# Turning a mixture's tokens and slot rows by VectorE and SBUF transfers, and three evictions given to ScalarE

## The chip, the cores and the metric

The kernel runs on one core of a Trainium2 chip. The metric is the device time of one execution in microseconds (us). A core has five engines that run their own instruction queues in order and wait for each other by semaphores: TensorE (PE; its weight loads are shown as PEld), VectorE (DVE), ScalarE (ACT), GpSimd (POOL) and SyncE (SP), which in this kernel issues every transfer (DMA). SBUF is the on-chip memory; TensorE writes its results to PSUM, from which VectorE or ScalarE moves them (an eviction).

## What is computed

Two layers over x of shape (2, 1024, 256) in fp32, each of a cross-attention to a context of 64 rows and a feed-forward, with a residual sum around each:

```python
x = x + L0_xattn(layernorm(x), ctx)   # 8 heads, softmax within 4 windows of 16 keys
x = x + L0_ffn(layernorm(x))          # 8 groups of 256 tokens: (x W1^T + b1) W2^T + b2
x = x + L1_xattn(layernorm(x), ctx)   # 16 heads of 16, sigmoid scores
x = x + L1_ffn(layernorm(x))          # mixture, below

# L1_ffn(x): slot_embeds of shape (8, 128, 256) = 1024 slot rows
xn = rms_norm(x, gamma_x);  se = rms_norm(slot_embeds, gamma_slot)
logits = einsum('bsd,etd->bset', xn, se)
dispatch = softmax(logits, axis=1)             # over the tokens
slots = einsum('bsd,bset->betd', xn, dispatch)
processed = gelu(slots @ w1) @ w2
combine = softmax(logits over all 1024 slots)  # over the slots
out = einsum('bnd,bsn->bsd', processed, combine)
```

The change concerns the way to logits: the product over d needs both tokens and slot rows with d on the partitions, so both are transposed ("turned").

## The kernel before

The 2048 tokens are held as four quads (q = 0 to 3, two to a batch), each a tile x of 128 partitions x 4 token tiles x 256. Stages follow each other:

- **Layer 0** (to about 107 us). The eight groups' weight pairs are multiplied ahead into one 256x256 matrix each (`product`, L522, tile pmt), with bias sums by VectorE (`bias_rows`, L553, tile b2z). Between the products stand `weigh` (scores psc L729, maximum mx L739, difference e L741, exponential L746, weights at L751), `attend` (transposes pat L760 of the weights, their eviction atT L762, product po L767, sum into x L775), `norm_ff` and `feed_forward` (po L580, POOL's bias sum L574, sum into x L587).
- **Layer 1's attention** (about 107 to 176 us). Keys and values are made once and evicted into kblk (L862) and vblk1 (L885). Then for every quad q and each of two chunks c: scores psg (L957, four banks), tanh by ScalarE (L966, tile sg), and, after what the code puts in between, the product poT (L996) and its eviction oT (L1003). In between stand the next quad's layer norm (`layernorm`, transposes pt_a L125) and queries (pq L897), the last quad's output (pf L911, sum into x L919), and the mixture's preparation.
- **The mixture's preparation.** `norm_slots` makes the slot rows' sums of squares (ScalarE, L826), their square root by POOL's pow (L829), and scales the rows by VectorE (L834). `turn_slot_rows(dc, h)` transposes four 128x128 blocks on TensorE (pse L842) and evicts them with the product of the two gammas into seT (L843). `norm_tokens(q)` takes moments by VectorE, powers by POOL (L117, L159), a few small VectorE operations (L160 to L165) and four scalings (L169) into xh. `turn_tokens(q)` transposes eight blocks on TensorE (pt_m L180) and evicts them by ScalarE and VectorE into xhT (L150, L152).
- **Logits** (about 170 to 236 us). Unit u = 0 to 15 is a tile of 128 tokens: four products pl (L196; each fp32 product is two instructions), VectorE's minimum and running maximum (L204, L211, L215), ScalarE's exponential ec (L219). Quads 0 to 3 are read from u = 0, 4, 8 and 12 on. `largest` (L254) and `spread` (L273) make the slot maxima's rows mb, and POOL adds them (`less`, L278).
- **Slots, hidden layer, combine** (236 us to the end), for each batch: `gather` (psl L289), `hidden` (pmh L364), `processed` (pp L430), `combine` (pc L455, sum into x L462, output L466). Meanwhile `turn` turns the exponentials ec by VectorE's 32x32 block transposes (L236, tile tr) and 16 transfers within SBUF (L243), each of 32 partitions; the weights ms are loaded (L1050).

The order of instructions on each engine is planned at build time by the library: it simulates the program with its own estimates and takes, of the instructions that are ready in its simulation, the one that comes first in the program. `nc.any` leaves the choice between ScalarE and VectorE to it. From the end of layer 1 on ScalarE follows the program's order. `tc.keep_in_program_order(i)` lets i be queued only behind the instruction that stands before it in the program on the same engine; it adds no wait. PSUM tiles come from two rotations (sides) of four banks.

Of the kernel before, what the change touches and what calls it, by code (L numbers as in the profile page):

```python
# [21 lines left out]
QT = 4  # L22
# [28 lines left out]
def tile_kernel(  # L51
# [10 lines left out]
    wff_in: bass.AP,  # L62
    b2: bass.AP,
    gammas: bass.AP,
    w1_in: bass.AP,
# [28 lines left out]

    gxs = const.tile([P, 2, DC], FP, name="gxs")
    gx, gs = gxs[:, 0, :], gxs[:, 1, :]
    ggx = const.tile([P, DC], FP, name="ggx")

# [6 lines left out]
    )  # L105
    seT = const.tile([P, DC, NSLOT], FP, tag="seT", name="seT")

    def moments(xt, name):

        st = stat.tile([P, QT, 6], FP, tag="bn", name=f"bn_{name}")  # L110
        mv = stat.tile([P, QT, 2], FP, tag="mv", name=f"mv_{name}")
        for t in range(QT):
            nc.vector.bn_stats(st[:, t, :], xt[:, t, :])
            nc.vector.bn_aggr(mv[:, t, :], st[:, t, :])
        rstd = stat.tile([P, QT], FP, tag="rstd", name=f"rstd_{name}")
        nc.gpsimd.tensor_scalar(rstd, mv[:, :, 1], LN_EPS, None, ALU.add)
        nc.gpsimd.tensor_tensor(rstd, rstd, m_half, ALU.pow)  # L117
        return mv, rstd

    def transposed(src, dst, name, side=0):  # L120

        for c in range(DC):
            pt = bank(f"pt_{name}_{c}", side)
            for t in range(QT):
                nc.tensor.transpose(pt[:, ts(t, P)], src[:, t, ts(c, P)], ident)  # L125
            nc.any.tensor_copy(dst[:, c, :], pt)


# [24 lines left out]

    def norm_tokens(q):

        mv, rstd = moments(xq[q], f"m_{q}")

        f = stat.tile([P, QT], FP, tag="f", name=f"f_{q}")
        nc.gpsimd.tensor_tensor(f, mv[:, :, 1], p_half, ALU.pow)  # L159
        nc.vector.tensor_scalar(f, f, float(D) ** 0.5, None, ALU.mult)  # L160
        nc.vector.tensor_tensor(f, f, rstd, ALU.mult)
        nc.vector.tensor_scalar(f, f, RMS_EPS, None, ALU.max)
        nc.vector.reciprocal(f, f)
        nc.vector.tensor_tensor(f, f, rstd, ALU.mult)
        nc.vector.tensor_scalar(f, f, float(D) ** 0.5, None, ALU.mult)  # L165
        xh = keep[q // QB].tile([P, QT, XW], FP, tag=f"xh_{q % QB}", name=f"xh_{q}")
        nc.gpsimd.memset(xh[:, :, D:XW], 1.0)
        for t in range(QT):
            nc.vector.tensor_scalar(  # L169
                xh[:, t, 0:D], xq[q][:, t, :], mv[:, t, 0:1], f[:, t : t + 1],  # L170
                ALU.subtract, ALU.mult,
            )
        xhs[q] = xh

    def turn_tokens(q):
        xhT = pools["mw"].tile([P, DC, QN], FP, tag="xhT", name=f"xhT_{q}", bufs=2)
        for c in range(DC):
            pt = bank(f"pt_m_{q}_{c}", 1)
            for t in range(QT):
                nc.tensor.transpose(pt[:, ts(t, P)], xhs[q][:, t, ts(c, P)], ident)  # L180
            copy(c, xhT[:, c, :], pt)
        xhTs[q] = xhT

    def logits(b, s):
# [8 lines left out]
        for n in range(NSLOT // 512):  # L193
            pl = bank(f"pl_{b}_{s}_{n}", 0)
            for dc in range(DC):
                nc.tensor.matmul(  # L196
                    pl,
                    lhsT=xhTs[q][:, dc, ts(t, P)],
                    rhs=seT[:, dc, ts(n, 512)],
                    start=(dc == 0),  # L200
                    stop=(dc == DC - 1),
                )
# [265 lines left out]
    with (  # L468
# [5 lines left out]
        se = w1p.tile([P, EC, D], FP, name="se")  # L474

        NCT, NPE = DC * 2 * B * NK, DC * NK
        fr = w1p.tile([P, NCT + NPE + NG * OC], FP, name="fr")
# [113 lines left out]
        def load_layer1():  # L591
            nc.sync.dma_start(out=w1s, in_=w1_in)
            nc.sync.dma_start(out=se, in_=slots_in)
            nc.sync.dma_start(out=gxs, in_=gammas)

        with tc.tile_pool(name="p0", bufs=1) as p0, tc.tile_pool(name="a0", bufs=2) as a0:
# [159 lines left out]
            def attend(q):  # L756
# [4 lines left out]
                atT = a0.tile([P, QN], FP, tag="atT", name=f"atT_{q}")  # L761
                nc.any.tensor_copy(atT, pat)  # L762
                for i in range(2):
# [51 lines left out]
        with (  # L815
# [3 lines left out]

            def norm_slots():  # L820
                sq = a1c.tile([P, D], FP, name="sq")
                sn = a1c.tile([P, EC], FP, name="sn")
                p_half8 = a1c.tile([P, EC], FP, name="p_half8")
                nc.gpsimd.memset(p_half8, 0.5)
                for c in range(EC):
                    nc.scalar.activation(  # L826
                        sq, se[:, c, :], AF.Square, accum_out=sn[:, c : c + 1]
                    )
                nc.gpsimd.tensor_tensor(sn, sn, p_half8, ALU.pow)  # L829
                nc.vector.tensor_scalar(sn, sn, RMS_EPS, None, ALU.max)  # L830
                nc.vector.reciprocal(sn, sn)
                nc.vector.tensor_scalar(sn, sn, float(D) ** 0.5, None, ALU.mult)
                for c in range(EC):
                    nc.vector.tensor_scalar(  # L834
                        se[:, c, :], se[:, c, :], sn[:, c : c + 1], None, ALU.mult
                    )
                nc.vector.tensor_tensor(ggx, gx, gs, ALU.mult)

            def turn_slot_rows(dc, h):
                pt = bank(f"pse_{dc}_{h}", 1)  # L840
                for c in range(4):
                    nc.tensor.transpose(pt[:, ts(c, P)], se[:, 4 * h + c, ts(dc, P)], ident)  # L842
                nc.vector.tensor_scalar(  # L843
                    seT[:, dc, ts(h, 512)], pt, ggx[:, dc : dc + 1], None, ALU.mult
                )

# [13 lines left out]
            for c in range(C1):  # L860
                for e in range(2):
                    nc.vector.tensor_scalar(  # L862
                        kblk[:, c, :, e, :],
                        pk[:, ts(c, P)].rearrange("p (b s) -> p b s", b=B),
                        parity[:, e : e + 1],
                        None,
                        ALU.mult,
                    )
# [14 lines left out]
            for e in range(2):  # L883
                r = slice(e * NK, (e + 1) * NK)
                nc.vector.tensor_copy(vblk1[r, :, :, e, :], pvv[r, :, :, e, :])  # L885

# [63 lines left out]
            for q in range(NQ):  # L950
                b = q * QN // S
                oTs[q] = a1.tile([P, C1, QN], FP, tag="oT", name=f"oT_{q}")
                for c in range(C1):
# [15 lines left out]
                    if c == 0:  # L969
# [11 lines left out]
                        if q > 0:  # L981
                            output(q - 1, (0, 1) if q + 1 < NQ else (0,))
                            turn_slot_rows(*divmod(q - 1, 2))
                        if q + 1 == NQ:
                            turn_tokens(0)
                    elif q + 1 < NQ:
                        queries(q + 1)
                        if q + 2 == NQ:
                            norm_tokens(0)
                            turn_slot_rows(1, 1)  # L990
                    else:
# [23 lines left out]
    for u in range(1, B * ST + 2):  # L1015
        b, s = divmod(u, ST)
        if b < B:
            if s % QT == 1:
                q = u // QT + 1
                if q < NQ:  # L1020
                    norm_tokens(q)
            logits(b, s)
            if s % QT == 2:
                q = u // QT + 1
                if q < NQ:
                    turn_tokens(q)
        v = u - ST
# [115 lines left out]
```

## Time and profile before

| | |
|---|---|
| median of 3 runs | 462.3 us (461.98 to 462.48) |
| profiled execution: time, span | 461.42 us, 459.6 us |
| TensorE busy | 446.4 us, 97% of the span |
| VectorE busy | 261.1 us, 57% |
| ScalarE busy | 110.8 us, 24% |
| POOL busy | 84.9 us, 18% |
| transfers | 38.61 MB, mean 84 GB/s |
| granted TensorE clock | 1.0 throughout |

A profile is one execution. "Busy" is the sum of an engine's instructions; the matmuls overlap each other, so the duration of one is longer than its distance from the next. The chain that ended last is followed back from the last instruction, at each step to what released it or to the instruction before it on its engine; it gives that distance. In the lists, L522 is line 522 of the kernel, "pmt<-wg" is output from input, and "idle" with an arrow names what ended an engine's wait.

### The profile page before, as it was taken

How to read it: one execution, taken by the hardware profiler on the slowest of the kernel's cores; microseconds unless marked ns; L12 is line 12 of the kernel's file. 1: busy time of each engine (PE TensorE's matmuls, PEld its weight loads, DVE VectorE, ACT ScalarE, POOL GpSimd, SP SyncE). 2: the span in 40 equal slices, each digit the busy share in tenths (PEclk: the TensorE clock that was granted, in tenths of full speed). 3: DMA queues.
4: the chain of work that ended last, by engine and by line, in shares of the span. 5: the costliest groups of instructions: out<-in, count | busy, mean ns of one | idle time of the engine just before them, and what ended most of it. 6: DMA issues, size and time to landing. Idle time of an engine off the chain costs nothing.

```text
span 459.6 us, 5446 instructions
## 1 busy us (share of the span) xinstructions
PE 446.4 (97%) x2032; PEld 322.2 (70%) x2032; DVE 261.1 (57%) x623; ACT 110.8 (24%) x205; POOL 84.9 (18%) x84
## 2 busy tenths in 40 slices
PE   6999897999999999999999999999999999999997
PEld 5788795888645555445458854688888874488886
DVE  0487889897256677987776279611331539911111
ACT  1212331211344441342573306300000003410000
POOL 3011332325111101100878910000000000000000
PEclk9999999999999999999999999999999999999999
DMA  8994691500000000000007534140252040430011
GB/s 287 411 429 198 260 427 45 185 0 1 1 1 0 2 0 1 0 0 1 0 1 227 89 52 72 33 80 0 52 98 36 12 79 1 82 102 1 11 47 35
DMA packets 74381, 38.61 MB, mean 84 GB/s; under 512 B 68465, under 2 KB 70641, under 8 KB 72945
## 3 DMA queue, kind: packets, MB, share of 16 engines
q1 hardware_dynamic: 74354, 38.26, 27.4%
q8 instruction: 16, 0.26, 0.2%
q14 instruction: 11, 0.09, 0.1%
HBM read 27.76 MB, written 2.10 MB: 65 GB/s over the span
## 4 chain that ended last, share of the span: by engine, by line
PE 82%; DVE 6%; POOL 1%; issue 0%
PE psl L289 12%; PE pc L455 12%; PE pp L430 12%; PE pl L196 11%; PE pmh L364 11%; PE pmt L522 6%; PE pq L897 3%; PE pf L911 3%; PE po L580 2%; PE psg L957 2%; PE poT L996 2%; DVE b2z L553 1%; DVE hn_f L486 1%; PE po L767 1%; PE pt_a L125 1%; PE pb L273 1%
## 5 line engine op out<-in xcount | busy, mean ns | idle before, releaser
L522 PE MATMUL pmt<-wg 128*128 128x256 f32 x256 | 60.1, 393 | 3.8 <-DMA wg<-in_wff_dram 3.8
L289 PE MATMUL psl<-xh,lg 128*128 128x258 f32 x256 | 58.7, 381 | 0.0
L522 PEld LDWEIGHTS pmt<-wg 128*128 128x128 f32 x256 | 49.9, 198 | 11.4 <-DMA wg<-in_wff_dram 4.3
L196 PE MATMUL pl<-seT,xhT 128*128 128x512 f32 x128 | 56.1, 592 | 0.0
L455 PE MATMUL pc<-pr,ec 128*128 128x256 f32 x256 | 55.6, 379 | 0.0
L430 PE MATMUL pp<-ms,mh 128*128 128x256 f32 x256 | 55.6, 379 | 0.0
L430 PEld LDWEIGHTS pp<-ms,mh 128*128 128x128 f32 x256 | 48.6, 190 | 7.5 <-DVE mh L408 0.5
L455 PEld LDWEIGHTS pc<-pr,ec 128*128 128x128 f32 x256 | 48.6, 190 | 6.6
L289 PEld LDWEIGHTS psl<-xh,lg 128*128 128x128 f32 x256 | 47.4, 190 | 7.2 <-issue 0.5
L196 PEld LDWEIGHTS pl<-seT,xhT 128*128 128x128 f32 x128 | 24.1, 190 | 27.9 <-issue 26.3
L278 POOL TENSOR_TENSOR lg<-lg,mb 128x1024 f32<-128x1024 f32 x16 | 37.2, 2366 | 32.3 <-ACT mb L150 27.9
L462 DVE SCALAR_TENSOR_TENSOR x<-pc,zc,x 128x256 f32<-128x256 f32 x16 | 7.7, 484 | 42.3 <-PE pc L455 42.3
L442 DVE COPY pr<-pp 128x512 f32<-128x512 f32 x8 | 5.5, 692 | 45.5 <-PE pp L430 45.5
L219 ACT ACTIVATE ec<-lg,nm 128x1024 f32<-128x1024 f32 x16 | 18.4, 1148 | 41.6 <-DVE nm L204 41.6
L398 ACT COPY mh<-pmh 128x512 f32<-128x512 f32 x8 | 4.6, 572 | 89.6 <-PE pmh L364 89.6
L374 ACT ACTIVATE mh<-mh 128x512 f32<-128x512 f32 x32 | 19.0, 626 | 21.1 <-DVE mh L408 16.1
L364 PE MATMUL pmh<-slT,ms 128*128 128x512 f32 x48 | 24.0, 592 | 0.0
L553 DVE SCALAR_TENSOR_TENSOR b2z<-wg,fr,b2z 128x256 f32<-128x256 f32 x48 | 23.6, 494 | 0.3
L297 DVE RECIPROCAL rz<-psl 128x1 f32<-128x1 f32 x16 | 2.6, 164 | 32.7 <-PE psl L289 32.7
L966 ACT ACTIVATE sg<-psg 128x512 f32<-128x512 f32 x32 | 16.5, 603 | 18.0 <-PE psg L957 18.0
L236 DVE STREAM_TRANSPOSE tr<-ec 128x512 f32<-128x512 f32 x32 | 20.1, 679 | 0.0
L281 ACT ACTIVATE lg<-lg 128x1024 f32<-128x1024 f32 x16 | 16.5, 1049 | 12.2 <-POOL lg L278 12.2
(169 smaller groups left out, 585.9 us busy)
## 6 DMA issues: line engine op xcount, KB each, us to landing
wg<-in_wff_dram SPq DMA_DIRECT2D x6, 2048.0 KB, 12.4
ec<-tr SPq DMA_DIRECT2D x128, 64.0 KB, 2.1
xT<-in_xT_dram SPq DMA_DIRECT2D x4, 512.0 KB, 13.4
x<-in_x_dram SPq DMA_DIRECT2D x4, 512.0 KB, 14.9
wg<-in_wff_dram SPq DMA_DIRECT2D x2, 1024.0 KB, 11.3
ms<-in_m_dram SPq DMA_DIRECT2D x1, 2048.0 KB, 8.3
out_dram<-x SPq DMA_DIRECT2D x16, 128.0 KB, 1.8
wg<-in_wff_dram SPq DMA_DIRECT2D x3, 512.0 KB, 6.0
```

What stands on the lines that cost most here:

```text
L196: nc.tensor.matmul(pl, lhsT=xhTs[q][:, dc, ts(t, P)], rhs=seT[:, dc, ts(n, 512)], start=(dc == 0), stop=(dc == DC - 1),)
L219: nc.scalar.activation(ecs[q][:, :, t, :], lg.rearrange("p (h n) -> p h n", h=2), AF.Exp, bias=nm[:, 1:2], scale=-1.0, accum_out=zcs[b][:, ...
L236: nc.vector.transpose(tr[:, :, :, t, :].rearrange("p r c n -> p c r n"), half[:, t, :].rearrange("p (c r n) -> p c r n", c=EC // 2, r=R4),)
L278: nc.gpsimd.tensor_tensor(lgs[b][s], lgs[b][s], mbs[b], ALU.add)
L281: nc.scalar.activation(lgs[b][s], lgs[b][s], AF.Exp, scale=-1.0)
L289: nc.tensor.matmul(pz[:, 0:XW], lhsT=lgs[b][s][:, ts(c, P)], rhs=xhs[b * QB + s // QT][:, s % QT, :], start=(s == 0), stop=(s == ST - 1),)
L364: nc.tensor.matmul(to, lhsT=lefts[i][:, ts(j, P)], rhs=slTs[b][:, i, 0:512] if i < 2 else rights[b][i], start=True, stop=True,)
L374: nc.scalar.activation(h, h, AF.Gelu)
L430: nc.tensor.matmul(pp[:, ts(k, D)], lhsT=hss[b, g, fc // 2][:, fc % 2, ts(2 * c2 + k, P)], rhs=m12s[1][:, fc, :], start=(fc == 0), stop=(f ...
L455: nc.tensor.matmul(pc[:, 0:D], lhsT=turned[:, c // 4, c % 4, t, :], rhs=prs[b, c // 4][:, c % 4, :], start=(c == 0), stop=(c == EC - 1),)
L522: nc.tensor.matmul(pm[:, ts(hc, D)], lhsT=w1g[:, oc, ts(hc, P)], rhs=w2g[:, oc, :], start=(oc == 0 and hc == 0), stop=(oc == OC - 1 and hc ...
L553: nc.vector.scalar_tensor_tensor(acc, weights[g][1][:, oc, :], b1s[:, g, oc : oc + 1], acc, ALU.mult, ALU.add)
```

## The change

Tokens and slot rows are no longer transposed on TensorE. A new helper `turned` does for 512 rows of 256 what `turn` does already for ec: four VectorE transposes of 32x32 blocks (128x256 each) into a tile tr, then 16 transfers within SBUF, issued by SP, that put the blocks in place (32 partitions x 8 runs of 128 bytes, 32 KB each). It is called four times for tokens and twice for slot rows, so the kernel has 24 more VectorE transposes and 96 more transfers, and 48 fewer TensorE transposes with their 12 evictions. Since nothing is evicted, the gammas go on the slot rows before: they are loaded as rows to all partitions (ggb), multiplied with each other and with each half of se by POOL; ScalarE scales the rows. seT is laid out half by half.

`norm_slots` and the slots' transposes are pinned in program order: behind the tanh of chunk (0,0), and behind layer 1's chunks (0,1) and (1,0). `norm_tokens` is split (`token_stats`); quads 0 and 1 are normed and turned in layer 1's chunks (1,1) and (2,1), quads 2 and 3 at logit units 1 and 3, and there is a third xhT buffer. Layer 1's keys and values, and layer 0's atT, are evicted by ScalarE. The host passes the gammas in two arrays: gx as before by partition, and both as rows.

```diff
     )
-    seT = const.tile([P, DC, NSLOT], FP, tag="seT", name="seT")
+    seT = const.tile([P, 2, DC, 512], FP, tag="seT", name="seT")
...
-        st = stat.tile([P, QT, 6], FP, tag="bn", name=f"bn_{name}")
-        mv = stat.tile([P, QT, 2], FP, tag="mv", name=f"mv_{name}")
+        st = stat.tile([P, QT, 6], FP, tag="bn" + name[0], name=f"bn_{name}")
+        mv = stat.tile([P, QT, 2], FP, tag="mv" + name[0], name=f"mv_{name}")
         for t in range(QT):
...
             nc.vector.bn_aggr(mv[:, t, :], st[:, t, :])
-        rstd = stat.tile([P, QT], FP, tag="rstd", name=f"rstd_{name}")
+        rstd = stat.tile([P, QT], FP, tag="rstd" + name[0], name=f"rstd_{name}")
         nc.gpsimd.tensor_scalar(rstd, mv[:, :, 1], LN_EPS, None, ALU.add)
...
+    def turned(src, dst, tr, late=False):
+        for t in range(QT):
+            turn = nc.vector.transpose(
+                tr[:, :, :, t, :].rearrange("p r c n -> p c r n"),
+                src[:, t, 0:D].rearrange("p (c r n) -> p c r n", c=DC, r=R4),
+            )
+            if late:
+                tc.keep_in_program_order(turn)
+        to = dst.rearrange("p c (t i n) -> p (c t) i n", t=QT, i=R4)
+        for i in range(R4):
+            for r in range(R4):
+                nc.sync.dma_start(
+                    out=to[ts(r, SQ), :, i, :],
+                    in_=tr[ts(i, SQ), r].rearrange("p c t n -> p (c t) n"),
+                )
...
-    def norm_tokens(q):
+    stats = {}
+    def token_stats(q):
         mv, rstd = moments(xq[q], f"m_{q}")
...
         nc.gpsimd.tensor_tensor(f, mv[:, :, 1], p_half, ALU.pow)
-        nc.vector.tensor_scalar(f, f, float(D) ** 0.5, None, ALU.mult)
+        stats[q] = mv, rstd, f
+    def norm_tokens(q):
+        if q not in stats:
+            token_stats(q)
+        mv, rstd, f = stats[q]
+        tc.keep_in_program_order(
+            nc.vector.tensor_scalar(f, f, float(D) ** 0.5, None, ALU.mult)
+        )
         nc.vector.tensor_tensor(f, f, rstd, ALU.mult)
...
     def turn_tokens(q):
-        xhT = pools["mw"].tile([P, DC, QN], FP, tag="xhT", name=f"xhT_{q}", bufs=2)
-        for c in range(DC):
-            pt = bank(f"pt_m_{q}_{c}", 1)
-            for t in range(QT):
-                nc.tensor.transpose(pt[:, ts(t, P)], xhs[q][:, t, ts(c, P)], ident)
-            copy(c, xhT[:, c, :], pt)
+        xhT = pools["mw"].tile([P, DC, QN], FP, tag="xhT", name=f"xhT_{q}", bufs=3)
+        tr = pools["mw"].tile([P, R4, DC, QT, SQ], FP, tag="tr", name=f"tr_m_{q}", bufs=2)
+        turned(xhs[q], xhT, tr)
         xhTs[q] = xhT
...
                     lhsT=xhTs[q][:, dc, ts(t, P)],
-                    rhs=seT[:, dc, ts(n, 512)],
+                    rhs=seT[:, n, dc, :],
                     start=(dc == 0),
...
+        ggb = w1p.tile([P, 2, D], FP, name="ggb")
         NCT, NPE = DC * 2 * B * NK, DC * NK
...
             nc.sync.dma_start(out=se, in_=slots_in)
-            nc.sync.dma_start(out=gxs, in_=gammas)
+            nc.sync.dma_start(out=gx, in_=gx_in)
+            nc.sync.dma_start(out=ggb, in_=gammas.partition_broadcast(P))
...
                 atT = a0.tile([P, QN], FP, tag="atT", name=f"atT_{q}")
-                nc.any.tensor_copy(atT, pat)
+                nc.scalar.copy(atT, pat)
                 for i in range(2):
...
             def norm_slots():
+                late = tc.keep_in_program_order
                 sq = a1c.tile([P, D], FP, name="sq")
...
                 p_half8 = a1c.tile([P, EC], FP, name="p_half8")
-                nc.gpsimd.memset(p_half8, 0.5)
+                late(nc.gpsimd.memset(p_half8, 0.5))
                 for c in range(EC):
-                    nc.scalar.activation(
-                        sq, se[:, c, :], AF.Square, accum_out=sn[:, c : c + 1]
+                    late(
+                        nc.scalar.activation(
+                            sq, se[:, c, :], AF.Square, accum_out=sn[:, c : c + 1]
+                        )
                     )
...
                 nc.vector.tensor_scalar(sn, sn, float(D) ** 0.5, None, ALU.mult)
+                gg = ggb[:, 0, :]
+                late(nc.gpsimd.tensor_tensor(gg, gg, ggb[:, 1, :], ALU.mult))
                 for c in range(EC):
-                    nc.vector.tensor_scalar(
-                        se[:, c, :], se[:, c, :], sn[:, c : c + 1], None, ALU.mult
-                    )
-                nc.vector.tensor_tensor(ggx, gx, gs, ALU.mult)
-            def turn_slot_rows(dc, h):
-                pt = bank(f"pse_{dc}_{h}", 1)
-                for c in range(4):
-                    nc.tensor.transpose(pt[:, ts(c, P)], se[:, 4 * h + c, ts(dc, P)], ident)
-                nc.vector.tensor_scalar(
-                    seT[:, dc, ts(h, 512)], pt, ggx[:, dc : dc + 1], None, ALU.mult
-                )
+                    nc.scalar.activation(
+                        se[:, c, :], se[:, c, :], AF.Copy, scale=sn[:, c : c + 1]
+                    )
+                for h in range(2):
+                    sh = se[:, ts(h, QT), :]
+                    nc.gpsimd.tensor_tensor(
+                        sh, sh, gg.unsqueeze(1).to_broadcast([P, QT, D]), ALU.mult
+                    )
+            def turn_slot_rows(h):
+                tr = lnp.tile([P, R4, DC, QT, SQ], FP, tag="tr", name=f"tr_se_{h}")
+                turned(se[:, ts(h, QT), :], seT[:, h], tr, late=True)
...
                 for e in range(2):
-                    nc.vector.tensor_scalar(
+                    nc.scalar.activation(
                         kblk[:, c, :, e, :],
                         pk[:, ts(c, P)].rearrange("p (b s) -> p b s", b=B),
-                        parity[:, e : e + 1],
-                        None,
-                        ALU.mult,
+                        AF.Copy,
+                        scale=parity[:, e : e + 1],
                     )
...
                 r = slice(e * NK, (e + 1) * NK)
-                nc.vector.tensor_copy(vblk1[r, :, :, e, :], pvv[r, :, :, e, :])
+                nc.scalar.copy(vblk1[r, :, :, e, :], pvv[r, :, :, e, :])
...
                             output(q - 1, (0, 1) if q + 1 < NQ else (0,))
-                            turn_slot_rows(*divmod(q - 1, 2))
-                        if q + 1 == NQ:
-                            turn_tokens(0)
+                        if q == 1:
+                            turn_slot_rows(1)
+                        if 0 < q < 3:
+                            token_stats(q - 1)
+                    if c == 1 and 0 < q < 3:
+                        norm_tokens(q - 1)
+                        turn_tokens(q - 1)
+                    if c == 0:
+                        pass
                     elif q + 1 < NQ:
                         queries(q + 1)
-                        if q + 2 == NQ:
-                            norm_tokens(0)
-                            turn_slot_rows(1, 1)
+                        if q == 0:
+                            turn_slot_rows(0)
                     else:
...
         if b < B:
-            if s % QT == 1:
-                q = u // QT + 1
-                if q < NQ:
-                    norm_tokens(q)
+            if u in (1, 3):
+                norm_tokens(QB + u // 2)
+                turn_tokens(QB + u // 2)
             logits(b, s)
-            if s % QT == 2:
-                q = u // QT + 1
-                if q < NQ:
-                    turn_tokens(q)
         v = u - ST
```

## The prediction

> **What bounds the kernel now.** I read the page's busy shares first, then TensorE's waits, then the chain that ended last, then the timelines of the engines that the change touches. Page, parts 1 and 2:
>
> ```profile
> PE 446.4 (97%) x2032; PEld 322.2 (70%) x2032; DVE 261.1 (57%) x623; ACT 110.8 (24%) x205; POOL 84.9 (18%) x84
> ...
> PE   6999897999999999999999999999999999999997
> ...
> PEclk9999999999999999999999999999999999999999
> ```
>
> TensorE is busy in 97% of the span, at the full granted clock. A busy row can hide short gaps, so I checked what TensorE waited for (us in total, times, longest):
>
> ```profile
> PE pmt L522 <- DMA wg<-in_wff_dram: 3.8, 1, 3.8
> PE po L767 <- DVE atT L762: 3.4, 1, 3.4
> PE pt_f L125 <- DVE e L741: 1.2, 1, 1.2
> PE pwk L686 <- ACT vblk L675: 1.0, 1, 1.0
> PE po L767 <- ACT atT L762: 0.7, 1, 0.7
> ```
>
> All of them lie before 73 us. The chain says the same: from 49.6 to 72.6 us it runs through VectorE, and from there nearly all is TensorE, back to back, to the last combine. So after 73 us each TensorE instruction that goes is worth its spacing, as long as nothing else comes late. The chain has the transposes that the change removes (start us, us, what):
>
> ```profile
> 160.35 0.44 PE pse L842 x4
> 160.78 0.99 PE poT L996 x8
> 161.78 1.07 PE psg L957 x8
> 162.85 2.01 PE pf L911 x8
> 164.86 0.44 PE pse L842 x4
> 165.30 0.87 PE pt_m L180 x8
> ```
>
> **Transposes off TensorE.** Four quads of tokens (pt_m x8 at 0.87 us) and four half-blocks of slot rows (pse x4 at 0.44) stand on the chain: 4 x 0.87 + 4 x 0.44 = 5.24 us, 0.109 each. The mean of 272 ns in the groups is a pipelined duration and would overstate it 2.5 times. **-5.2 us.**
>
> **atT by ScalarE.** The second wait above is this one (engine timelines, PE then DVE):
>
> ```profile
> 67.41 0.60 PE L760 MATMUL pat<-ident,at 128*128 128x128 f32 x4
> 67.85 1.46 PE L522 MATMUL pmt<-wg 128*128 128x256 f32 x6
> 72.67 1.99 PE L767 MATMUL po<-vw,atT 128*128 128x256 f32 x8 [3.36 <-DVE atT L762]
> ...
> 69.75 0.68 DVE L587 TENSOR_TENSOR x<-x,po 128x512 f32<-128x512 f32 x1
> ...
> 71.94 0.68 DVE L762 COPY atT<-pat 128x512 f32<-128x512 f32 x1
> ```
>
> pat is complete at 68.0, but the copy stands in VectorE's queue until 71.94. ScalarE is idle from 66.5 to 73.3; its three copies of this kind took 0.59 us. So atT is there at 68.6 and po can follow the six pmt at 69.3 instead of 72.67. Its second bank comes free when L587 ends at 70.43, while TensorE would want it at 70.2, so 3.36 shrinks to about 3.1. What is late next? TensorE reaches pat of quad 3 at 81.58 - 3.1 = 78.5, and its at (L751) ends at 77.3, so 1.2 us are left; the b2z sums of group 3 end near 61 and the weights were asked for long before. Bounds 0 (the planner spends it elsewhere) to 3.4. **-3.1 us.**
>
> **Keys and values of layer 1.** Six evictions move to ScalarE, which is idle from 107.8 to 110.5; at 0.26 (its 64x128 copies) to 0.38 us (128x256) they cost some 2 us, and their readers start at 118.9 (pvs) and 123.7 (psg). Nothing.
>
> **norm_slots, pinned behind the first tanh group.** It leaves the stretch of 62 to 102 us, where its 8 scalings (0.35 each) lay beside busy TensorE, and starts when tanh (0,0) ends, at 126.8 in before's time. Step by step: 8 Squares at 0.54 us spacing, to 131.1; POOL's pow 1.65, to 132.8; three small VectorE operations, to 133.5; ScalarE's scaled copies (Square's 0.32 spacing) with tanh (0,1), 2.06 us, in their way, four of them by about 136; POOL's multiplication by the gammas for a half, as L278 (same shape, 2.37), to 138.5; four VectorE transposes, half of L236's size, 0.36 each, to 140-141. Behind the Squares on ScalarE stands tanh (0,1), ready at 131.36, so just free. If ScalarE parks on a scaled copy ahead of tanh, poT (0,1), now at 135.0, would start at 133.4 + 2.6 + 2.06 = 138.1: 3.1 us late. If VectorE parks on the slot transposes, oT (0,1) behind them has 1.1 us of room before pf. That the planned order parks an engine on POOL is seen already: L160 and L161 held VectorE for 3.3 and 3.1 us over four token norms, 1.6 us a quad. Bounds 0 (or a little gain: VectorE loses 4 x 0.68, 4 x 0.75, 8 x 0.35, 4 x 0.34, 2 x 0.41 and 0.68, 11.4 us, and gets 24 x 0.36, 8.6) to 3.1; nearest is that 1.6 against the 1.1 of room, once or twice: **+1.0 us.**
>
> **POOL beside VectorE.** Two multiplications of 2.37 us enter. While POOL ran L574 (81.25, 1.35 us), a VectorE L553 took 1.50 instead of 0.48 us; while it ran L278 at 242.8 to 261.3, VectorE's transposes kept 668 to 712 ns. So transposes are free of it, and a one-source VectorE operation may lose 1 to 2 us off the path: nothing. The Trainium skill ("SBUF — State Buffer", section "SBUF: two separate sides") states an exclusive lock on a port pair that VectorE and GpSimd share, whoever starts first keeping it for the whole instruction, for VectorE in a two-port mode or with two SBUF inputs. The L553 row agrees; if the lock also took the new transposes, two multiplications would push them back by up to 4.7 us.
>
> **The transfers on SP.** What was one eviction becomes 16 transfers of 32 KB for each quad or half, 96 in all, on SP's one queue. The rows to price them (ns min/median/max):
>
> ```profile
> L243 SPq DMA_DIRECT2D ec<-tr x128: 585/627/1613, 245.5 to 401.4; - x128
> ...
> L466 SPq DMA_DIRECT2D out_dram<-x x16: 332/386/617, 402.1 to 457.1; - x16
> ...
> DMA to landing us min/median/max: 2.1/2.1/5.0
> ...
> L236 DVE STREAM_TRANSPOSE tr<-ec x32: 668/670/712, 242.5 to 390.7; 128x512 f32<-128x512 f32 x32
> ```
>
> L243 is the same pattern with twice the runs (512 of 128 B); L466 has 128 rows. A line through the two minima (585 at 512, 332 at 128) gives 0.42 us at 256; I take 0.45, with ends 0.33 and 0.63. The first logits need both slot halves and quad 0: 48 transfers from 141 on. At 0.45: 141 + 21.6 + 2.1 = 164.7. TensorE gets to pl at 170.0 less the transposes before it (4 x 0.44 + 0.87), 167.4: hidden, with 2.7 us to spare. All of this moves earlier together by the 3.1. At 0.63: 141 + 30.2 + 2.1 = 173.3, 5.9 us late, less what the planner moves ahead (poT of 1.0 and pf of 3.5 us remain). Quad 1 follows by 172-183, needed at 186; quad 2 by 193, needed near 198; quad 3 waits for the third xhT buffer's turn (about 187) and lands by 203, needed near 212. Behind them on SP stands only the load ms, which waited 161 us for L273 in any case. **0, bounds 0 to +5.9.**
>
> The skill speaks against this path: "VectorE: DVE Perf Modes", section "The three transpose paths", has VectorE transposing only 32x32 blocks, advises TensorE for a full 128x128, and calls a plain strided DMA copy a trap, 19 times slower than the crossbar's transposing transfer. Here a copy is 16 x 0.627 us for a megabyte, off TensorE's path; by the skill the sum would lose the 5.2 us and pay for transfers, so end above before.
>
> **Sum.** The profiled execution took 461.42 us (span 459.6), 0.9 below the median 462.3. 461.42 - 5.2 - 3.1 + 1.0 = 454.1; with the 0.9, **455.0 us**. About 0.2% (0.9 us) is what a measurement of this kernel can tell from no change.
>
> **Rivals.** *First logits wait for SP* (issue of 0.5 to 0.63 us): 1 to 6 us are given back: 457 to 461. For it: nearly every L243 takes over 0.6. Against: half the runs per transfer, and reordering. *The atT gain is lost*: 458.1. Against: 1.2 us of room is small, but VectorE is relieved. *Waits take the place of the removed work*, 0.63 us per transfer and no atT gain: 461.42 - 5.2 + 5.9, no difference. *Slower*: SP is the bound at the first logits. 8.3 us less the 1.0, and 0.9 more to be seen, are paid back if quad 0 lands 8.2 us after 167.4, at 175.6: from (175.6 - 2.1 - 141)/48 = 0.68 us per transfer if TensorE finds nothing else to do. That is just above L243's median, and its maximum is 1.61; at 0.85 us it would be 470. *It does not do what it says*: the pin holds an instruction behind only the one before it in the program, so the slot work may float forward to 63 us again; then transfers start earlier, the 1.0 goes, and 454 results, inside the forecast's case.
>
> **The numbers.** Forecast 0.57 (453 to 457, floating included), SP late 0.19, atT lost 0.06: faster 0.82. No difference 0.05. Slower 0.13. The range reaches from 453.0 (no new wait, 3.4 for atT, 0.7 of scatter and of the small early waits) to 461.0 (a wait of 5.9 at the first logits on top of the 1.0); it leaves out the last two cases, 0.18.
>
> **What would show it.** After: PE near 441 us busy; no pt_m or pse; no wait of po on atT over 1 us; the issue row of the new transfers at 0.42 to 0.5 us, 96 of them; TensorE's waits between 120 and 140 us about 1 us in sum; pl's first wait under 1 us. I am wrong if TensorE waits for xhT or seT by several us, if poT or pf wait for ScalarE or VectorE by more than 3 us, or if the 3.36 us reappear elsewhere before 80 us.

## The result and the profile after

The changed kernel takes 465.13 us (464.70 to 466.01) against 462.14 us (461.65 to 462.48) of the kernel before beside it: a ratio of 1.0068, 95% interval 1.005 to 1.0086. It is slower by 0.7%, where 455.0 us were forecast. The profiled execution took 464.70 us, span 462.8 us.

The page after, parts 1 and 2, in the rows that were read before:

```profile
PE 445.7 (96%) x1984; PEld 317.8 (69%) x1984; DVE 266.3 (58%) x625; ACT 113.4 (25%) x214; POOL 89.9 (19%) x87
...
PE   6999999999959999999999999999999999999997
...
PEclk9999999999988999999999999999999999999999
```

The 48 transposes are gone (2032 to 1984 instructions), yet TensorE is busy for only 0.7 us less. Two slices around 140 us have a granted clock under 0.9, and the first of them has a hole (five tenths busy). TensorE's waits name it (us in total, times, longest):

```profile
PE pmt L551 <- DMA wg<-in_wff_dram: 3.6, 1, 3.6
PE poT L1036 <- ACT sg L1001: 2.7, 1, 2.7
PE psg L992 <- DVE qT L939: 2.7, 1, 2.7
PE pf L946 <- DVE oT L1043: 1.7, 2, 1.0
```

The wait of po for atT (3.4 us before) is not there any more, nor is that of pt_f for e (1.2). Three new ones are, all in layer 1's attention; two smaller new ones are po's for x (0.8 in two) and pb's for dg (0.7, below). To find where the time went, the same instruction is looked up in both traces. After minus before, in us:

| start of | before | after | difference |
|---|---|---|---|
| scores psg of chunk (0,0) | 123.62 | 118.95 | -4.7 |
| psg (0,1) | 130.22 | 125.54 | -4.7 |
| psg (1,0) | 135.91 | 139.56 | +3.7 |
| psg (1,1) | 142.90 | 147.73 | +4.8 |
| end of layer 1's last pf | 179.44 | 184.24 | +4.8 |
| end of the last logits pl | 235.44 | 237.64 | +2.2 |
| span | 459.6 | 462.8 | +3.2 |

Up to chunk (0,1) the change is 4.7 us ahead. 1.0 of it stood there from the program's first loads on, which differ from execution to execution (0.9 in the run with atT alone, below, whose code is that of before up to there); 1.1 is pt_f's wait for e, which is gone in every run below that turns the slot rows the new way and stays in the two that don't; most of the rest, 2.3, is atT. That one chunk then loses 8.3 us, and the next 1.2, although it has one transpose group (0.44) less. From the last pf to the last pl 2.6 are given back, as the three quads of pt_m there promised (3 x 0.87). Near the end 1.0 is lost again.

The loss is read from four timelines of this chunk. Timelines after of PE, ACT, DVE and POOL (start us, us, what; in brackets the idle time before and its releaser):

```profile
126.61 3.70 PE L932 MATMUL pq<-hT_a,w1s 128*128 128x512 f32 x8
130.25 1.04 PE L1036 MATMUL poT<-sg,vblk 128*32 128x512 f32 x2
134.01 2.88 PE L1036 MATMUL poT<-sg,vblk 128*32 128x512 f32 x6 [2.72 <-ACT sg L1001]
139.56 1.21 PE L992 MATMUL psg<-qT,kblk 32*128 32x512 f32 x8 [2.68 <-DVE qT L939]
...
126.73 0.60 ACT L1001 ACTIVATE sg<-psg 128x512 f32<-128x512 f32 x1
130.17 3.30 ACT L870 ACTIVATE se<-se,sn 128x256 f32<-128x256 f32 x8 [2.85 <-DVE sn L866]
133.38 1.54 ACT L1001 ACTIVATE sg<-psg 128x512 f32<-128x512 f32 x3
...
128.18 0.69 DVE L864 TENSOR_SCALAR sn<-sn 128x8 f32<-128x8 f32 x1 [3.04 <-POOL sn L863]
129.98 0.16 DVE L866 TENSOR_SCALAR sn<-sn 128x8 f32<-128x8 f32 x1
130.50 0.18 DVE L114 BATCH_NORM_AGGREGATE mv_a<-bn_a 128x2 f32<-128x6 f32 x1
132.16 5.44 DVE L515 TENSOR_SCALAR hn_a<-x,mv_a,rstd_a 128x256 f32<-128x256 f32 x4 [1.47 <-POOL rstd_a L117]
137.52 1.41 DVE L134 STREAM_TRANSPOSE tr_se<-se 128x256 f32<-128x256 f32 x4
138.85 0.65 DVE L939 COPY qT<-pq 128x512 f32<-128x512 f32 x1
...
126.50 1.65 POOL L863 TENSOR_TENSOR sn<-sn,p_half 128x8 f32<-128x8 f32 x1 [5.54 <-ACT sq L859]
132.09 4.71 POOL L875 TENSOR_TENSOR se<-se,ggb 128x1024 f32<-128x1024 f32 x2
```

Read ACT first. Of the four tanh of chunk (0,1) one is done; then the queue holds the eight scalings of the slot rows, and they wait 2.85 us for sn: POOL computes its square root until 128.15, and the last of VectorE's three small operations on it, which are queued among moments and an eviction, ends at 130.14. The other three tanh, with scores ready in PSUM, stand behind them and come at 133.38. TensorE stops in the middle of poT. On VectorE the layer norm hn of a later quad, four operations of 0.41 us elsewhere, takes 5.44 us: it starts at 132.16, and POOL's two multiplications by the gammas run from 132.09 to 136.80. Behind hn stand the slot transposes and then the copy of the queries qT, which TensorE needs next: the second stop of 2.7 us.

The clock is the third part. The windows view after, in stretches of 3.40 us (granted clock third from the end of each row):

```profile
130.25:133.65 3.40, 1.04 (x3) 0.13 (x2) 1.89 (x3) 3.40 (x9) 2.79 (x3) 1.00 0.01 2
133.65:137.05 3.40, 2.88 (x6) 0.55 (x6) 3.40 (x3) 1.74 (x4) 3.15 (x2) 0.50 0.00 0
137.05:140.45 3.40, 0.89 (x8) 0.31 (x8) 3.11 (x8) 0.00 (x0) 0.00 (x0) 0.99 0.02 3
140.45:143.85 3.40, 3.40 (x16) 2.88 (x13) 0.69 (x1) 2.54 (x5) 0.00 (x0) 0.51 0.36 54
143.85:147.25 3.40, 3.40 (x22) 2.42 (x20) 2.07 (x6) 0.00 (x0) 0.00 (x0) 0.99 0.34 50
```

After each of the two stops TensorE works one stretch at half clock. So the 8.3 us of the chunk are 2.7 + 2.7 of waits and 2.9 in poT itself (3.92 us for its eight, 0.99 before: split, fed tanh by tanh, and at half clock); the half clock from 140.45 costs the next chunk 1.6 (8.17 us against 6.99 less the 0.44).

The transfers, by the lines of their tile (ns min/median/max, first and last start), and VectorE's dg near the end, first before, then after:

```profile
L143 SPq DMA_DIRECT2D xhT<-tr_m x64: 585/609/807, 160.1 to 212.5; - x64
L143 SPq DMA_DIRECT2D seT<-tr_se x32: 585/609/739, 139.0 to 159.4; - x32
```

```profile
L259 DVE TENSOR_TENSOR dg<-ident,mT x2: 1221/1224/1226, 214.9 to 238.5; 128x1024 f32<-128x1024 f32 x2
```

```profile
L286 DVE TENSOR_TENSOR dg<-ident,mT x2: 1221/1736/2251, 218.2 to 240.7; 128x1024 f32<-128x1024 f32 x2
```

A transfer costs 0.61 us (0.66 from one start to the next), not 0.45. TensorE never waits for one. The second dg takes 2.25 instead of 1.22 us: it now starts at 240.65, while POOL's `less` of the first batch runs to 241.81; before, POOL was done at 238.36 and dg started at 238.45. TensorE waits 0.7 us for it. That is the 1.0 lost near the end.

### The profile page after: what moved, and what is told of

Same layout as the page of the kernel before. It is cut to its first block, busy times and chain, and to the rows that moved or that the text cites. A ratio compares the mean times of both kernels' runs of the same rounds, so it can differ in the third digit from the quotient of the medians.

```text
span 462.8 us, 5514 instructions
## 1 busy us (share of the span) xinstructions
PE 445.7 (96%) x1984; PEld 317.8 (69%) x1984; DVE 266.3 (58%) x625; ACT 113.4 (25%) x214; POOL 89.9 (19%) x87
## 4 chain that ended last, share of the span: by engine, by line
PE 80%; DVE 12%; POOL 2%; ACT 2%; issue 1%; DMA 1%; ACTq 0%; POOLq 0%
PE pc L482 12%; PE pp L457 12%; PE psl L316 11%; PE pl L223 11%; PE pmh L391 10%; PE pmt L551 9%; PE pf L946 3%; DVE b2z L582 2%; PE po L609 2%; DVE oT L1043 1%; PE psc L759 1%; ACT sq L859 1%; PE pb L300 1%; DVE hn_f L515 1%; PE pvw L734 1%
## 5 line engine op out<-in xcount | busy, mean ns | idle before, releaser
L582 DVE SCALAR_TENSOR_TENSOR b2z<-wg,fr,b2z 128x256 f32<-128x256 f32 x48 | 24.6, 516 | 0.5
```

What stands on the lines that cost most here:

```text
L582: nc.vector.scalar_tensor_tensor(acc, weights[g][1][:, oc, :], b1s[:, g, oc : oc + 1], acc, ALU.mult, ALU.add)
```

## The experiments

The theory: the pins put the slot norm's chain (POOL's root, scalings, gammas) into chunk (0,1), where ScalarE parks on it ahead of tanh and VectorE is held by POOL ahead of qT. The rivals: the evictions of layer 1's keys and values on ScalarE, the new layout itself with its transposes on VectorE, or the transfers are the cost. Ratios are to the kernel before, with 95% intervals.

**Without the slot pins** (the change; `norm_slots` and the slot transposes may float; the pin on token norms stays):

```diff
-                late = tc.keep_in_program_order
+                late = lambda i: i
...
-                turned(se[:, ts(h, QT), :], seT[:, h], tr, late=True)
+                turned(se[:, ts(h, QT), :], seT[:, h], tr)
```

> The changed kernel without the pins of the slot norm and the slot transposes: the planner floats both forward to about 62 to 105 us, and the 32 transfers of the slot rows start there. Theory (the pins put the chain of ScalarE, POOL and VectorE into the two chunks where TensorE has no room, and everything else of the change works): psg (0,0) to psg (1,0) takes 12.3 us as before instead of 20.6, the clock stays at 1.0, no wait of TensorE over 1 us after 75 us, the first logits find xhT there. 462.1 - 5.2 - 3.1 = 453.8, up to 2 us more if POOL's multiplications hold up VectorE's b2z sums: 454.5 us (453.5 to 457). Rival (VectorE, already busy to 90% between 60 and 100 us, becomes the bound there): 458 to 464 us.

454.28 us (453.91 to 454.53), ratio 0.9837 [0.9825, 0.9850]. The slot work goes back to 61 to 104 us. The page and TensorE's waits, all of this kernel:

```profile
PE 441.1 (97%) x1984; PEld 316.1 (70%) x1984; DVE 265.5 (59%) x624; ACT 114.1 (25%) x215; POOL 90.5 (20%) x87
```

```profile
PE pf L946 <- DVE oT L1043: 0.7, 1, 0.7
PE pb L300 <- DVE dg L286: 0.7, 1, 0.7
PE pv L910 <- DVE bs L590: 0.3, 1, 0.3
```

From psg (0,0) to psg (1,0) it takes 12.29 us again, exactly the time before. Each against the runs of before beside it, the change loses 3.0 us and this kernel gains 7.5: the pins cost 10.5 us, and everything else in the change brings 7.5.

**Only the pins of the slot norm removed** (the first two lines of the diff above; the slot transposes stay pinned).

> The changed kernel; only the pins of the slot norm are taken away, the slot transposes stay pinned. Theory (it is the slot norm's chain over ScalarE, POOL and VectorE, put into the chunk where nothing has room, that costs the time; transposes whose input is long there hold up nothing): as without any pin, 454.5 us (453.8 to 455.5); SP gets the second half's 16 transfers near 138, quad 0's by 148 to 158.5, and the first logits do not wait. Rival (pinned transposes and 48 transfers close together make the first logits wait): 456 to 459 us.

455.45 us, ratio 0.9872 [0.9857, 0.9887]. It gains 6.2 us on the runs of before beside it, so 9.2 of the 10.5 us belong to the norm's pins. Those of the transposes cost the rest, 1.3 us; TensorE's waits show 1.0 of it (pf waits for oT 1.7 us in two, as in the change, against 0.7 in one without any slot pin).

**Scalings on VectorE** instead of ScalarE, pins kept: ScalarE can't park on them.

```diff
-                    nc.scalar.activation(
-                        se[:, c, :], se[:, c, :], AF.Copy, scale=sn[:, c : c + 1]
+                    nc.vector.tensor_scalar(
+                        se[:, c, :], se[:, c, :], sn[:, c : c + 1], None, ALU.mult
```

> The changed kernel, with the eight scalings of the slot rows by VectorE in place of ScalarE; POOL's two multiplications stay. Theory (two parks in a row: ScalarE holds tanh (0,1) behind scalings that wait for sn, then VectorE stands behind POOL): the wait of poT for sg, 2.7 us, goes, and both qT copies come back to ScalarE, so psg (1,0) starts near 131.5 instead of 139.6; but oT (0,1) still stands on VectorE behind the slot transposes and the layer norm of quad 3, whose power is behind POOL's multiplications, until about 139.5, so that pf waits 5 to 7 us there. Net gain only 2 to 3 us: 462.6 us (461.5 to 464). Rival A (ScalarE's park alone is the cause): 457 us. Rival B (the transfers or VectorE's transposes as such cost the time): no change, 465 us.

464.07 us, ratio 1.0053 [1.0042, 1.0065]: the wait for tanh goes, but the gain does not come. Timelines of this kernel, PE, DVE and POOL:

```profile
141.97 5.64 PE L946 MATMUL pf<-w1s,oT 128*128 128x256 f32 x14 [6.70 <-DVE oT L1043]
...
131.82 4.29 DVE L870 TENSOR_SCALAR se<-se,sn 128x256 f32<-128x256 f32 x8
136.03 0.17 DVE L114 BATCH_NORM_AGGREGATE mv_a<-bn_a 128x2 f32<-128x6 f32 x1
136.12 1.39 DVE L134 STREAM_TRANSPOSE tr_se<-se 128x256 f32<-128x256 f32 x4
139.88 1.38 DVE L515 TENSOR_SCALAR hn_a<-x,mv_a,rstd_a 128x256 f32<-128x256 f32 x4 [2.37 <-POOL rstd_a L117]
141.18 0.74 DVE L1043 TENSOR_SCALAR oT<-poT,vsum 128x512 f32<-128x512 f32 x1
...
136.19 2.34 POOL L875 TENSOR_TENSOR se<-se,ggb 128x1024 f32<-128x1024 f32 x1 [0.76 <-DVE se L870]
138.50 0.22 POOL L116 TENSOR_SCALAR rstd_a<-mv_a 128x4 f32<-128x4 f32 x1
```

The two stops became one of 6.7 us. The scalings push the last aggregate of the layer norm (136.03) back, so its power on POOL falls behind both multiplications, hn waits for that, and oT for hn. The expectation had this wait right (5 to 7 us) and missed the time by 1.5 us. It had no price for the clock: from 139.95 to 146.75, two stretches of 3.4 us, the granted clock is 0.50, and the fourteen pf take 5.64 us, against 3.29 for fourteen in the change at 157.05.

**Without the gammas** (pins and ScalarE's scalings kept; POOL's two multiplications of se left out, so the logits lack the product of the two gammas):

```diff
-                for h in range(2):
-                    sh = se[:, ts(h, QT), :]
-                    nc.gpsimd.tensor_tensor(
-                        sh, sh, gg.unsqueeze(1).to_broadcast([P, QT, D]), ALU.mult
-                    )
```

> The changed kernel without POOL's two multiplications of the slot rows by the gammas (this factor of the logits is left out); the scalings stay on ScalarE. Theory (two parks): the four hn scalings of VectorE fall from 5.4 us to 1.4, qT is copied by 135 us and psg (1,0) starts when poT (0,1) ends, near 137 instead of 139.6; the wait of poT for sg stays at 2.5 to 3 us. 465.1 - 2.6, and 0.9 less for VectorE's later largest/dg if the clock recovers: 462.3 us (461 to 463.5). Rival A (POOL's hold on VectorE is the whole cause): the wait for sg goes too, 457 us. Rival B (transfers): no change, 465 us.

461.33 us, ratio 0.9987 [0.9976, 0.9997], 3.8 us below the change. The wait for qT is gone and the one for tanh stays (2.7). The lines of hn by source line, first with the multiplications (the change), then without:

```profile
L515 DVE TENSOR_SCALAR hn_a<-x,mv_a,rstd_a x16: 401/410/2437, 82.4 to 137.2; 128x256 f32<-128x256 f32 x16
```

```profile
L515 DVE TENSOR_SCALAR hn_a<-x,mv_a,rstd_a x16: 370/407/412, 82.9 to 135.0; 128x256 f32<-128x256 f32 x16
```

Without POOL beside it no hn takes over 0.41 us. With the second stop one of the two stretches at half clock goes too (mean granted clock 0.996 against 0.993). This separates the two stops: POOL makes the second, ScalarE's park the first.

**One VectorE operation for scaling and gammas**, with the pins and without them:

```diff
-                    nc.scalar.activation(
-                        se[:, c, :], se[:, c, :], AF.Copy, scale=sn[:, c : c + 1]
-                    )
-                for h in range(2):
...
+                    nc.vector.scalar_tensor_tensor(
+                        se[:, c, :], se[:, c, :], sn[:, c : c + 1], gg, ALU.mult, ALU.mult
+                    )
```

> The changed kernel with all its pins; scaling and gammas of the slot rows in one VectorE operation per block (x8), so that neither ScalarE nor POOL has a part behind the power. Theory: both parks as they were go (no wait of poT for sg, none of psg for qT), but VectorE still waits for the power and does 3.9 us of scalings, 1.4 of transposes and 1.4 of hn before oT (0,1): pf waits about 3 us; SP starts at 135 and quad 0 lands near 168.5, about when TensorE wants it: 459 us (457.5 to 461). Rival (ScalarE and POOL were the whole cause): 454 to 455.5 us.

462.39 us, ratio 1.0020 [1.0011, 1.0028]. It takes away both causes found so far, no tanh and no qT is late, and still nothing is gained over before: pf waits 4.75 us. Timelines of this kernel, PE, DVE, POOL:

```profile
139.56 4.78 PE L941 MATMUL pf<-w1s,oT 128*128 128x256 f32 x14 [4.75 <-DVE oT L1038]
...
131.35 3.24 DVE L870 SCALAR_TENSOR_TENSOR se<-se,sn,ggb 128x256 f32<-128x256 f32 x8
134.51 1.42 DVE L134 STREAM_TRANSPOSE tr_se<-se 128x256 f32<-128x256 f32 x4
135.85 0.14 DVE L114 BATCH_NORM_AGGREGATE mv_a<-bn_a 128x2 f32<-128x6 f32 x1
137.46 1.38 DVE L515 TENSOR_SCALAR hn_a<-x,mv_a,rstd_a 128x256 f32<-128x256 f32 x4 [1.47 <-POOL rstd_a L117]
...
136.08 0.23 POOL L116 TENSOR_SCALAR rstd_a<-mv_a 128x4 f32<-128x4 f32 x1 [6.27 <-DVE mv_a L114]
```

The order is the planner's: one aggregate of 0.14 us is queued behind 4.66 us of slot work, POOL's power waits for it, and oT stands behind hn. The expectation (459 us) missed by 3.4: it had about 3 us for this wait and nothing for the clock, which is 0.50 from 139.56 to 142.00, so that the fourteen pf take 4.78 us and not 3.29.

> The same fused scaling without any pin. Theory: as the version without pins, the chain lying beside TensorE's products; VectorE gets 1.1 us more between 75 and 100 us and loses POOL's hold: 454.0 us (453.3 to 455). Rival (VectorE is the bound between 75 and 105 us): over 456 us.

Without pins it is 454.42 us, ratio 0.9843 [0.9830, 0.9857], the same as the kernel that only lost its pins. Where the slot norm is free, these two ways to split it between engines take the same time.

**Before with atT alone on ScalarE** (`nc.any.tensor_copy(atT, pat)` becomes `nc.scalar.copy(atT, pat)`, nothing else):

> The kernel before, with atT alone evicted by ScalarE. Theory (the gain of the first part is real and comes from atT): TensorE's wait of 3.36 us for atT shrinks to under 1 us and everything after 73 us moves forward with it, 462.1 - 3.1 = 459.0 us (458.5 to 459.5). Rival (the changed kernel's earlier start of layer 1, 4.7 us at the first psg, comes from moving the slot norm out of the way and from the start, not from atT): 461.5 to 462.5 us.

461.94 us, ratio 1.0009 [1.0001, 1.0018]: no gain at all. The wait of po falls from 3.36 to 0.31 us as forecast, and TensorE is 3.9 us ahead at 106 us (0.9 of it from the first loads, as said above). Then (timelines of this kernel, PE and DVE; windows view):

```profile
105.92 1.04 PE L125 MATMUL pt_a<-ident,hn_a 128*128 128x128 f32 x8
109.69 8.62 PE L522 MATMUL pmt<-wg 128*128 128x256 f32 x31 [2.73 <-issue]
...
108.48 1.11 DVE L862 TENSOR_SCALAR kblk<-pk,parity 128x128 f32<-128x128 f32 x4
```

```profile
110.10:113.50 3.40, 3.40 (x10) 2.69 (x9) 2.37 (x6) 0.00 (x0) 1.04 (x1) 0.50 0.02 5
113.50:116.90 3.40, 3.40 (x18) 2.99 (x17) 0.00 (x0) 0.00 (x0) 0.00 (x0) 1.00 0.00 0
```

The last product needs the PSUM bank that holds the keys pk, and VectorE evicts them only by 109.59. The view names no releaser ("issue"), but the times fit to 0.1 us: in the kernel before, that eviction ends at 110.81 and the product starts at 110.92, so there was no room there either. 2.7 us of the 3.9 are waited off, the half clock takes 1.7 more.

**Before with all three evictions on ScalarE** (atT, kblk and vblk1, as in the diff of the change):

> The kernel before, with atT and also layer 1's keys and values evicted by ScalarE. Theory (atT's 3.4 us come forward as far as product 7, whose bank is the one of pk and waits for VectorE's eviction into kblk; with ScalarE doing that the gain stays): TensorE's wait of 2.7 us before product 7 goes and 458.6 us results (458.0 to 459.3). Rival (something else that VectorE does by then, the layer norm or bias of the group, holds product 7): 461 to 462 us as with atT alone.

457.70 us, ratio 0.9914 [0.9901, 0.9928]. The wait is gone, the product starts at 107.73, and 3.9 us are gained by the times of the runs; in the two traces psg (0,0) starts 3.2 us earlier (120.37) and the span is 3.2 us shorter. No wait of the kernel before names the evictions of keys and values; they are what lets the gain of atT through.

**Twice as many transfers of half the size** (without slot pins; each in two of 16 KB):

```diff
-                nc.sync.dma_start(
-                    out=to[ts(r, SQ), :, i, :],
-                    in_=tr[ts(i, SQ), r].rearrange("p c t n -> p (c t) n"),
-                )
+                for k in range(2):
+                    nc.sync.dma_start(
+                        out=to[ts(r, SQ), ts(k, QT), i, :],
+                        in_=tr[ts(i, SQ), r, k],
+                    )
```

> The version without pins, with each turned block moved by 32 transfers of 16 KB in place of 16 of 32 KB (the same bytes). It takes the place of a test of SP's queue, which no version so far has made late. Theory (a transfer costs SP about 0.65 us whatever its size, as 0.609 for 256 runs against 0.627 for 512 says): 20.9 us a quad; quad 0 lands near 169 against 164.4 wanted, 4.5 us of waiting at the first pl, then about 2, 7 and 7 us at the quads 1 to 3: 475 us (468 to 480). Rival (the price goes with the runs, 0.33 to 0.4 us at 128 runs): 454 to 458 us.

471.06 us, ratio 1.0206 [1.0185, 1.0228]. TensorE's waits, and the transfers by their source line, of this kernel:

```profile
PE pl L224 <- DMA xhT<-tr_m: 12.9, 4, 7.5
```

```profile
L144 SPq DMA_DIRECT2D xhT<-tr_m x128: 585/599/1458, 145.7 to 229.6; - x128
L144 SPq DMA_DIRECT2D seT<-tr_se x64: 586/599/1353, 102.3 to 144.5; - x64
```

Half the bytes, the same price: SP pays per transfer. With 96 transfers the logits never wait, with 192 they wait in all four quads, 12.9 us in sum. The time is 16.8 us longer than with 96; the mean granted clock fell as well, from 0.999 to 0.984.

**Token norms and turns behind oT** (without slot pins; the calls for quads 0 and 1 moved behind the chunk's poT and oT):

```diff
-                    if c == 1 and 0 < q < 3:
-                        norm_tokens(q - 1)
-                        turn_tokens(q - 1)
...
                         oTs[q][:, c, :], po, 0.5, vsum[:, c, b : b + 1], ALU.mult, ALU.add
                     )
+                    if c == 1 and 0 < q < 3:
+                        norm_tokens(q - 1)
+                        turn_tokens(q - 1)
```

> The version without pins, with the norm and the turning of quads 0 and 1 placed after the chunk's poT and oT rather than before. Theory (oT is behind VectorE's token norm and transposes, and pf waits 0.7 to 1.0 us for it): that wait goes and quad 0 still lands in time, 453.7 us (453.0 to 454.5), 0.1 to 0.2% below the version without pins. Rival (the token norm then comes late for the first logits): 455 to 458 us.

454.18 us, ratio 0.9833 [0.9818, 0.9848]. The wait of pf for oT goes, but the time is that of the kernel without pins within the uncertainty. The three versions without any slot pin beat both kernels: 1.6 to 1.7% below before, 2.2 to 2.3% below the change; with the transposes' pins kept it is 1.3% below before.

## Why the prediction was wrong

The forecast missed by 10 us and on the other side of no change. The steps, one by one:

- **norm_slots, pinned (+1.0, bounds 0 to 3.1): the step that failed.** The timing of its chain was good: sn complete at 133.5 less the 4.7 is 128.8, measured 130.1 (POOL was on time, VectorE's three small operations were not). Both parks were named as well. Wrong was the sizing: I took the 1.6 us of a token norm's park against 1.1 us of room "once or twice". The trace has two stops in a row, 2.7 us by ScalarE and 2.7 by VectorE, 2.9 more in the split product and 1.6 of half clock: 9.9 us. The runs without the pins show this term's size: 9.2 us for the norm's, 10.5 for all. The upper bound of 3.1 counted one park and stopped there; it should have added them up, since a stop of one engine doesn't shelter the next.
- **POOL beside VectorE (nothing).** I had the row (0.48 to 1.50 us beside POOL) and put the loss off the path. It fell on hn, which nobody needs soon, but qT's copy is queued behind hn, and the next scores need that: 3.8 us by the run without the multiplications. I also took only the transposes (rightly: in the run without pins two lay beside POOL, at 94.62 and 96.04, and took 0.43 us; in the change none did) and did not ask which other operations of VectorE would lie beside 4.7 us of POOL, or that `nc.any` would put qT's copy on VectorE. The Trainium skill ("SBUF — State Buffer", section "SBUF: two separate sides") has the lock held for the whole instruction; the row of 2.44 us for one hn beside multiplications of 2.4 us agrees with that, where my "1 to 2 us" did not follow it through.
- **atT (-3.1) and keys and values (nothing).** The sum of both was right (3.9 us by the times of the runs with these alone, 3.2 in their traces), the split was not: alone atT brings nothing. In the change atT brought 2.3, since po then waits twice for x (0.8 us), and the 1.1 of pt_f's wait for e made up for it: the forecast had that row and no term for it, so this was luck, and no run says why the wait went. The question "what is late next" stopped at quad 3, at 78.5 us; the next thing late was a PSUM bank 30 us further on.
- **Transposes (-5.2).** Right. From psg (0,0) to the end of the last pl the kernel before takes 111.82 us and the one without slot pins 107.57 (119.66 to 227.23): 4.25 us less, although a wait of pf for oT (0.7) stands in it that came with the change; without that it is 4.9.
- **Transfers (0, at 0.45 us).** Hidden as forecast, at a wrong price: 0.61 us, the upper end. The line through 512 and 128 runs was no law, as runs don't set the price. In the change quad 0 landed near 160.1 + 16 x 0.66 + 2.0 = 172.7 for a first pl at 174.80, and that was 4.8 us late itself; without the pins it lands near 158.6 for 164.38. That the pinned kernel would have been held by SP if nothing else had been late is arithmetic; no run shows it.
- **The rivals.** The slower one had the right sign and the wrong mechanism: SP decides from 0.68 us per transfer, and at 0.61 (0.66 from one start to the next) it did not. "The pin does not hold, 454" is what the runs without pins measure (454.28). The missing rival was the two parks in series: at 3.1 each it would have been 454.1 - 1.0 + 6.2 = 459.3 in the profiled execution, and 462.7 with 1.7 for each stretch at half clock, which only these runs show.
- **The signs named beforehand** were the right ones to look at: waits of about 1 us between 120 and 140 us (measured 5.4), and TensorE near 441 us busy (445.7, and 441.1 without the slot pins).

## What to carry to other kernels

A pin in program order keeps work from being done early, and here it made ScalarE and VectorE wait in line for it; before pinning a chain that crosses engines, write down for each of its links what stands behind it in that engine's queue, and add up the stops, since here two of 2.7 us became 9.9. Work that was off the critical path and early cost nothing here, but the same work beside short-lived PSUM results stopped TensorE through the instruction queued behind it, however small. A gain of some us in the middle of this kernel lasted only if the next shared resource (a PSUM bank that VectorE empties) had the same room; look for instructions that start just as their input is ready.

## What was not expected of the hardware

**The clock falls after short stops, and on a grid.** In the change the granted clock is 0.50 in 133.65 to 137.05 and 0.51 in 140.45 to 143.85, and about 1.0 in the stretches before, between and after: steps of 3.4 us. The stop that led to the first was 2.72 us long, and filled 2.4 us of the stretch ahead; in the run with atT alone one of 2.73 us cost the same 3.4 us at 0.50, 1.7 us of work. Yet the kernel before stops for 3.36 us at 69.3 and keeps 1.00 in the profiled execution. That is not so in all of them: of its 23 runs beside the one with atT alone, 17 have a mean granted clock of 0.996, about what one stretch of 3.4 us at half clock makes of 460 us (1.7/460 = 0.004), and 6 have 1.0, with a span 0.6 us shorter in the mean. The kernel without the gammas has ten runs at 0.996 and one at 1.0, and that one's span is 457.5 us where the ten have 459.0 to 460.3. So the same kernel loses the clock in one execution and keeps it in another; which stop did it in the runs without a trace is not shown. The Trainium skill ("TensorE: Matmul & The Clock Gate", section "What's actually happening") has a free-running window of 3413 ns that throttles after at least one idle window. The window's length agrees with the rows; that it must be wholly idle does not, since TensorE was busy for 1.04 and 0.89 us in the stretches ahead of the two drops. A stop that straddles two windows would leave each half busy, which would explain the 3.36 us, but as the clock did not move there, the trace can't show where the windows lay. A stop of 2.7 us should be priced at 2.7 to 4.4 us.

**The price of a transfer on SP** is 0.59 to 0.63 us in the median whether it moves 16, 32 or 64 KB within SBUF (0.599, 0.609, 0.627).
